# Scores of a two-layer cross-attention block: float32 products replaced by groups of float32r products on high and low parts

## The chip, the cores and the metric

The kernel runs on one core of one Trainium2 chip. The metric is the device time of one execution in microseconds, the median over several executions; lower is better. The core has a matrix engine (TensorE, PE in the profile; its weight loads are PEld), a vector engine (VectorE, DVE), an activation engine (ScalarE, ACT), a general engine (GpSimd, POOL) and SyncE (SP), whose queue issues nearly all of the DMAs here.

## The reference

Two layers, all in float32. Each layer does self attention, cross attention and a gated feed-forward on `x` of 4 x 512 x 320, with 20 heads of 16 dimensions; cross attention reads a context of 4 x 1601 x 192.

```
h1 = _ln(x, n1_g, n1_b)
x = _attn(h1, h1, q1, k1, v1, o1_w, o1_b, heads) + x
h2 = _ln(x, n2_g, n2_b)
x = _attn(h2, context, q2, k2, v2, o2_w, o2_b, heads) + x
h3 = _ln(x, n3_g, n3_b)
a, g = jnp.split(h3 @ ff_w1 + ff_b1, 2, axis=-1)
return a * jax.nn.gelu(g, approximate=False) @ ff_w2 + ff_b2 + x
```

`_attn` is `softmax(q k^T / 4) v` for each head, followed by the output projection.

## The kernel before, in words

**Units.** The work of a layer is cut into units. An attention unit is one batch entry and one group of four heads: 20 units of self attention, then 20 of cross attention, then four feed-forward units (one a batch entry); then the same for the second layer. A self unit has 4 chunks of 128 keys, a cross unit 13 (the last has 65 keys). Units are counted from 0 in order; layer 0 has self units 0 to 19, cross units 20 to 39 and feed-forward units 40 to 43, layer 1 has 44 to 63, 64 to 83 and 84 to 87.

**Rows.** Queries and keys of a unit lie transposed in SBUF, dimensions on partitions. Each head of the four has 32 rows: 16 hold its dimensions, one more holds a constant (keys) or minus the row maximum (queries), so that one product of 32 rows gives `q k - max`. The four heads stand on the four row groups of TensorE, so their products run side by side.

**A chunk** (function `main`). `score` multiplies keys by queries into a PSUM bank (line 1077), ScalarE takes the exponential (line 1083), and one chunk later `values` multiplies by the values (line 1097); ScalarE copies the result out (line 1113) and GpSimd adds it up (line 1114). Between these, the chunk computes part of the row maxima of the unit that follows: `max_pairs` gives products of queries and keys for two heads at a time (line 906, and line 930 for the 65 last keys), and VectorE reduces two banks at once (line 922). One product group for two heads is called here a half round, for all four heads a round. A self unit needs 4 rounds (8 halves), a cross unit 13 (26 halves). When all are there, `max_end` turns the maxima with VectorE (line 970) and eight small DMAs on SP's queue put them in the query rows (line 977).

**Who is served when.** Program order is written by a small planner while the program is built. A clock counts two ticks ("rounds of the clock") a chunk, so unit `u` begins at tick `u.start`, 8 ticks (self) or 26 ticks (cross) after the one before. Side work (projections, normalisation, values, output projection) waits in chains with due times. `steps` runs once at the end of a chunk and takes from the chains what is due and what a credit allows. The chain "slots" holds the transfers that put keys in their rows: `steps` sets `clock["slots"] = 1`, and each entry taken lowers it, so one entry a chunk is taken at most.

**Half rounds of maxima** are handed out by `give`, twice a chunk. It looks at the next two units. If a unit's data has been in place for 3 ticks (`at_hand`), it gives one half round to the chunk. It also counts what is owed: if units would not be done in time, `owed` grows, and each whole unit owed becomes an extra round behind the chunk's own products. Five ticks before a unit begins, what is still left is urgent:

```
if left(v) and (rest == 1 or alone and rest < 1):
    urgent = urgent or v
    owed = max(owed, 1.0 if alone and rest > -4 else (left(v) + 1) // 2)
owed += most * went if total else 0.0
while owed >= 1.0 and any(left(v) for v in ahead) and not (alone and rounds and rest > -4):
```

(`rest` is `v.start - 4 - tick`; `most` is then `(left - 1) / 2`.) Each pass of this loop takes the first unit with something left and calls `at_once(v)`, which projects what is missing and issues the transfers that are still queued.

**Keys of a cross unit** come from `keys_of_context` into a stage, and four queue entries later (lines 773 and 774) by DMA in their rows; queries and the keys of a self unit are put in rows by GpSimd (line 647). Units are projected three ahead (`add_proj`), due at `lead(u) - 6`, where `lead(u)` is the start of the unit before; keys of a cross unit 10 ticks before that. The function `free` keeps a key buffer until its last reader is done.

Of the kernel before, what the change touches and what calls it, by code (L numbers as in the profile page):

```python
# [9 lines left out]
F32 = mybir.dt.float32  # L10
I32 = mybir.dt.int32
# [8 lines left out]
FF = 4 * D  # L20
# [10 lines left out]
HEAD = [0, 2, 1, 3]  # L31
AUG = [DH, DH, 0, 0]
# [34 lines left out]
def kernel(ctx: ExitStack, tc: tile.TileContext, x, context, ws, out):  # L67
# [25 lines left out]
    three = ctx.enter_context(tc.tile_pool(name="three", bufs=3))  # L93
    prs = ctx.enter_context(tc.tile_pool(name="prs", bufs=9))
# [9 lines left out]
    slots = ident.rearrange("p (j s) -> p j s", s=SLOT)  # L104
    keep, ones = [], []
    for b in range(2):
        k, o = (const.tile([P, 1], F32, name=f"{n}{b}") for n in ("keep", "ones"))
        nc.vector.tensor_reduce(k, slots[:, :, b * DH : (b + 1) * DH], AX.XY, ALU.add)
        nc.vector.tensor_reduce(o, slots[:, :, AUG[2 * b]], AX.X, ALU.add)
        keep.append(k)  # L110
        ones.append(o)
# [6 lines left out]
    nmax = []  # L118
    for i in range(2):
        m = const.tile([P, SLOT], F32, name=f"nmax{i}")  # L120
        nc.gpsimd.memset(m, 0.0)
        nmax.append(m)


    kbuf = [const.tile([P, 4 * QT + P], F32, name=f"kT{i}") for i in range(3)]
    qbuf = [const.tile([P, N], F32, name=f"q{i}") for i in range(4)]
    fill = qbuf[3]
    nc.vector.memset(fill, 1.0)

    blank = kbuf[0][:, 4 * QT :]

    def blanks(k):

        n = k.shape[-1] // P
        of = blank.rearrange("p (o w) -> p o w", o=1)
        return [
            lambda a=a, b=min(a + 5, n): dma(
                out=k.rearrange("p (a w) -> p a w", w=P)[:, a:b], in_=of.to_broadcast([P, b - a, P])  # L140
            )
            for a in range(0, n, 5)
        ]


    kept = []
    for b in range(2):
        k = const.tile([P, 1], F32, name=f"kept{b}")
        nc.vector.tensor_scalar(k, keep[b], DH**-0.5, None, ALU.mult)
        kept.append(k)  # L150
    zero = const.tile([P, 1], F32, name="zero")
    nc.vector.memset(zero, 0.0)
    nc.gpsimd.memset(blank, 0.0)
    for b in range(2):
        rows = slice(b * GD, (b + 1) * GD)
        nc.gpsimd.tensor_scalar(blank[rows], blank[rows], zero[rows], ones[b][rows], ALU.mult, ALU.add)
# [16 lines left out]
    wq1, wk1, wv1, wq2 = (wpool.tile([P, 3, D], F32, name=n) for n in ("wq1", "wk1", "wv1", "wq2"))  # L173
# [9 lines left out]
    w1r = wpool.tile([P, FF], F32, name="w1r")  # L183
    w2 = wpool.tile([P, NHC, D], F32, name="w2")
# [57 lines left out]
    def load_ff(l):  # L242
# [5 lines left out]
        def last_rows(half):  # L248
            dma(
                out=w1r[half * REST : (half + 1) * REST, :],  # L250
                in_=ws[l]["ff_w1"][2 * P :, half * FF : (half + 1) * FF],
            )
# [5 lines left out]
            + [lambda c=c: dma(out=w2[:, c], in_=second[:, c]) for c in range(NHC)]  # L258
# [12 lines left out]
    class Unit:  # L271


        def __init__(self, l, kind, b, g):
# [5 lines left out]
            self.cols = [c * P for c in range(self.nch)]  # L280
            if self.cross:
                self.cols = [c % 4 * QT + c // 4 * P for c in range(self.nch - 1)] + [4 * QT]
            self.keyed = False
            self.kslots = deque()
            self.kwhen = None
# [9 lines left out]
            self.pairs = self.hT = self.q = self.kvT = None  # L295
# [15 lines left out]
    for i, u in enumerate(attn):  # L311
# [7 lines left out]
        u.kT = kbuf[(u.m + 1) % 3 if u.cross else 0]  # L319
        u.k0 = 0 if u.cross else u.m % 3 * N  # L320
        u.qbuf = qbuf[3 if u.early else i % 3]
# [327 lines left out]
    def add_proj(u):  # L649
        wq, wk = wq2 if u.cross else wq1, wk1  # L650
# [5 lines left out]
        tiles = [  # L656
            (
                i,
# [796 lines left out]
```

## Time and profile before

| | |
|---|---|
| median of 3 runs | 3196.92 us (3194.64 to 3197.47) |
| span of the profiled execution | 3195.3 us |
| the profiled execution's own time | not given apart from its span; the span lies 1.6 us under the median of the runs |
| busy: PE, PEld, DVE, ACT, POOL | 3163.1, 1466.6, 2069.2, 1972.4, 1204.1 us |
| DMA | 77.84 MB, mean 24 GB/s |

Busy time is the union of an engine's instructions. A float32 matmul stands in the profile as two instructions, each with a weight load of its own, so 2720 scores are 5440 rows. Lines of a view give the source line, the engine, the operation, what it writes and reads, and how often it stands there.

### The profile page before, as it was taken

To read this page: it belongs to the slowest core of one execution; us is meant where nothing else is said; L and a number is where in the kernel's file an instruction comes from. 1 tells how busy PE (TensorE), PEld (TensorE's weight loads), DVE (VectorE), ACT (ScalarE), POOL (GpSimd) and SP (SyncE) were. 2 spreads that over 40 slices of the span, in tenths; PEclk is the share of its full clock that TensorE was granted. 3 is DMA by queue.
4 is the path that set the end of the run, shared out by engine and by line. 5 is a ranking of instruction groups with operands and counts; after the bars stand their busy time and mean duration, and the time that the engine had idled before them with its cause. 6 is when DMAs were issued, how large, how long until landed. Compare 5 with 4: busy or idle time off the path is not lost. (4 is left out here: it accounts for less than half of the span.)

```text
span 3195.3 us, 81370 instructions
## 1 busy us (share of the span) xinstructions
PE 3163.1 (99%) x33970; PEld 1466.6 (46%) x33970; DVE 2069.2 (65%) x2662; ACT 1972.4 (62%) x3951; POOL 1204.1 (38%) x1617
## 2 busy tenths in 40 slices
PE   9999999999999999999999999999999999999999
PEld 4444444444444444355444444444444444443555
DVE  7787777778678677422247777777777777773221
ACT  4666577777777777611147665777778777785110
POOL 5555334443443443301135553344434444432000
PEclk9999999999999999999999999999999999999999
DMA  2220011100100100100012100010010010001000
GB/s 67 56 70 17 14 26 39 33 21 19 33 21 20 33 16 11 39 6 0 1 30 61 34 14 14 22 28 16 16 32 10 16 33 9 16 11 37 9 11 15
DMA packets 104851, 77.84 MB, mean 24 GB/s; under 512 B 42908, under 2 KB 95012, under 8 KB 104484
## 3 DMA queue, kind: packets, MB, share of 16 engines
q1 hardware_dynamic: 104400, 72.63, 9.3%
q8 instruction: 268, 4.39, 0.6%
q14 instruction: 99, 0.81, 0.1%
q0 software_dynamic: 64, 0.00, 0.0%
q10 hardware_dynamic: 20, 0.00, 0.0%
HBM read 33.04 MB, written 7.93 MB: 13 GB/s over the span
## 5 line engine op out<-in xcount | busy, mean ns | idle before, releaser
L1083 ACT ACTIVATE pr<-st 128x512 f32<-128x512 f32 (+1 forms) x2720 | 1408.6, 602 | 420.7 <-PE sps L906 360.4
L1077 PE MATMUL st<-q,kT 32*128 32x512 f32 (+1 forms) x5440 | 1362.6, 614 | 2.6 <-DVE nmax L922 1.7
L922 DVE TENSOR_REDUCE pm<-sps 128x2 f32<-128x1024 f32 (+1 forms) x974 | 1134.4, 1203 | 268.9 <-PE sps L906 262.4
L906 PE MATMUL sps<-kT,q 32*128 32x512 f32 x5120 | 1275.7, 621 | 14.2 <-DVE nmax L922 9.8
L1114 POOL TENSOR_TENSOR o<-o,vo 128x512 f32<-128x512 f32 x576 | 734.5, 1275 | 1375.8 <-ACT vo L1113 1200.7
L1077 PEld LDWEIGHTS st<-q,kT 32*128 32x128 f32 (+1 forms) x5440 | 503.8, 181 | 517.4 <-ACT pr L1083 291.1
L1097 PE MATMUL av<-pr,vals 128*32 128x512 f32 (+1 forms) x5440 | 729.3, 605 | 0.3
L922 DVE TENSOR_REDUCE nmax<-sps 128x2 f32<-128x1024 f32 (+1 forms) x338 | 378.5, 1160 | 151.7 <-PE sps L906 149.1
L906 PEld LDWEIGHTS sps<-kT,q 32*128 32x128 f32 x5120 | 406.1, 183 | 125.8 <-issue 80.6
L1113 ACT COPY vo<-av 128x512 f32<-128x512 f32 x576 | 339.8, 590 | 45.2 <-PE av L1097 41.1
L1097 PEld LDWEIGHTS av<-pr,vals 128*32 128x32 f32 (+1 forms) x5440 | 110.0, 108 | 493.4 <-ACT pr L1083 480.2
L1199 PE MATMUL fps<-hT,w 128*128 128x512 f32 x640 | 286.1, 600 | 1.0 <-DVE kT L1223 0.5
L1222 ACT ACTIVATE gl<-fps,b 128x512 f32<-128x512 f32 x80 | 50.7, 684 | 371.0 <-PE fps L1212 268.0
L647 POOL TENSOR_SCALAR q<-qst,keep,zero 64x128 f32<-64x128 f32 (+1 forms) x476 | 232.3, 488 | 58.9 <-ACT qst L711 25.5
L1199 PEld LDWEIGHTS fps<-hT,w 128*128 128x128 f32 x640 | 119.2, 191 | 152.1 <-issue 146.9
L699 PE MATMUL qps<-hT,wq 112*32 112x128 f32 (+3 forms) x2880 | 126.8, 310 | 0.5 <-DVE pm L922 0.5
L1024 PEld LDWEIGHTS ops<-wo,aT 112*32 112x32 f32 (+1 forms) x3072 | 98.4, 110 | 62.2 <-issue 32.5
L1223 DVE SCALAR_TENSOR_TENSOR hid<-fps,b,gl 128x512 f32<-128x512 f32 x48 | 33.8, 746 | 143.0 <-ACT gl L1222 143.0
L438 POOL TENSOR_SCALAR root<-root 128x4 f32<-128x4 f32 x23 | 5.3, 230 | 315.5 <-DVE root L432 314.8
L1024 PE MATMUL ops<-wo,aT 112*32 112x160 f32 (+1 forms) x3072 | 123.9, 299 | 0.2
L699 PEld LDWEIGHTS qps<-hT,wq 112*32 112x32 f32 (+1 forms) x2880 | 86.7, 110 | 79.3 <-issue 38.8
L1260 DVE TENSOR_TENSOR x<-yps,x 128x320 f32<-128x320 f32 x32 | 15.7, 492 | 148.5 <-PE yps L1253 148.5
(88 smaller groups left out, 2255.7 us busy)
## 6 DMA issues: line engine op xcount, KB each, us to landing
kT<-kst SPq DMA_DIRECT2D x320, 48.0 KB
aT<-o SPq DMA_DIRECT2D x320, 32.0 KB
q<-turned SPq DMA_DIRECT2D x636, 1.0 KB
w<-in_L_xattn_ff_w_dram SPq DMA_DIRECT2D x20, 256.0 KB
ctxT<-ctxT SPq DMA_DIRECT2D x24, 208.0 KB
ctxT<-ctxT SPq DMA_DIRECT2D x12, 416.0 KB
ctxin<-in_ctx_dram SPq DMA_DIRECT2D x24, 192.0 KB
w<-in_L_xattn_ff_w_dram SPq DMA_DIRECT2D x20, 160.0 KB
```

Of the source, the lines that this page charges most:

```text
L647: nc.gpsimd.tensor_scalar(to, stage[rows, :w], keep[b][rows], more[rows], ALU.mult, ALU.add)
L699: nc.tensor.matmul(ps[to, :w], lhsT=wq[:n, k, gs], rhs=first.hT[:n, k, at[i] : at[i] + w], start=(k == 0), stop=(k == 2),)
L906: nc.tensor.matmul(ps, lhsT=u.q[j * SLOT : (j + 1) * SLOT, t * P : (t + 1) * P], rhs=u.kT[j * SLOT : (j + 1) * SLOT, u.k0 + s * 512 : u.k0 ...
L922: nc.vector.tensor_reduce(to[:, j : j + n], part, AX.X, ALU.max, negate=(ns == 1))
L1024: nc.tensor.matmul(ps[f : f + m, : D // 2], lhsT=aT[:n, k, t * P + f : t * P + f + m], rhs=wo[:n, k, cols], start=(k == 0), stop=(k == 2),)
L1077: nc.tensor.matmul(st[:r, :], lhsT=u.kT[rows, u.k0 + u.cols[c] : u.k0 + u.cols[c] + r], rhs=u.q[rows, :], start=True, stop=True)
L1083: nc.scalar.activation(p[:r], st[:r], AF.Exp)
L1097: nc.tensor.matmul(ps[i * SLOT : (i + 1) * SLOT, :], lhsT=columns_of[:r, head : head + SLOT], rhs=pr.pop((c, j))[:r, :], start=True, stop= ...
L1113: nc.scalar.copy(vo, ps)
L1114: nc.gpsimd.tensor_tensor(u.o, u.o, vo, ALU.add)
L1199: nc.tensor.matmul(ps, lhsT=w1[:, k, i * FF + c * P : i * FF + (c + 1) * P], rhs=u.hT[:, k, :], start=ahead and k == 0, stop=not ahead and ...
L1222: nc.scalar.activation(gl, pss[1], AF.Gelu, bias=b1[:, NHC + c : NHC + c + 1])
```

## The change

Queries and keys are cut into two parts each: `high`, rounded to float32r, and `low`, the difference. The 32 rows of a head hold both parts of its 16 dimensions. Keys hold (high, low); queries are held twice, as (high, low) and as (low, high), so that two float32r products give all four part products. Minus the row maximum has moved out of the rows to tiles of its own (`nrows`, two rows a head), which a third float32r product with two rows of ones adds. A score is therefore three products, a product for the maxima two. `round_of` now lays the products of a whole chunk in five steps: heads 0 and 1 have their three scores in steps 0 to 2, heads 2 and 3 in steps 2 to 4, and the products for the maxima fill the other row groups.

The parts reach their rows by way of DRAM: the projection is copied out by ScalarE, GpSimd makes the two parts (`split`), DMAs write them to `q_way` or `k_way`, and DMAs read them back in rows. These are `moves`: five for a self unit (write keys, write queries, read keys, read queries twice), eight for a cross unit. Each move has one entry in the chain "slots". The first two units are moved by hand (`at_once`) before the main loop. Queries and keys of a self unit are projected together (`both`), due at `lead(u) - 9`. A projection waits until earlier moves have left its way buffer (`way_free`). `w1r`, `w2`, the hidden layer and these buffers now share space, and `w2` is loaded later.

```diff
+    def split(low, high):
+        nc.gpsimd.tensor_copy(high.bitcast(F32R), low)
+        nc.gpsimd.tensor_tensor(low, low, high, ALU.subtract)
...
-        due = lead(u) - 6
+        due = lead(u) - 9
         keys_due = due - 10 if u.cross else due
...
+        def move(pairs, then=None, what=None, may=yes):
+            def f():
+                if what:
+                    pending[what] -= 1
+                u.moving = clock["round"]
+                for i, (to, of) in enumerate(pairs):
+                    queue = (nc.sync, nc.scalar, nc.gpsimd)[i % 3] if start["on"] and u.i == 0 else nc.sync
+                    queue.dma_start(out=to, in_=of)
+                if then:
+                    then()
...
+        def way_free(what):
+            return not pending[what] and (len(users[what]) < 2 or not users[what][-2].moves)
...
+        def both(part):
...
+                nc.tensor.matmul(
+                    ps[:, :w],
+                    lhsT=wqk[:n, k, u.g].rearrange("p i d -> p (i d)"),
+                    rhs=first.hT[:n, k, at : at + w],
...
+                nc.scalar.activation(low[:, at : at + w], ps[:, :w], AF.Copy, scale=scales[:, 0:1])
...
+            if u.i:
+                split(low, high)
+            move([(to_k[:, 0], high[GD:]), (to_k[:, 1], low[GD:])], what="q")
+            move([(to_q[:, 0], high[:GD]), (to_q[:, 1], low[:GD]), (to_q[:, 2], high[:GD])], what="q")
+            move([(u.kT[:, u.k0 : u.k0 + N].bitcast(F32), by_rows(to_k))], may=free)
+            read_queries(to_q)
...
+        def add_moves(n, due):
+            for _ in range(n):
+                add(
+                    "slots", 0.0, lambda: u.moves and u.moves.popleft()[0](), due,
+                    lambda: u.moves[0][1]() if u.moves else u.when is not None,
+                    lambda: clock["slots"] > 0 and clock["round"] >= u.moving + 2,
+                )
+        if not u.cross:
+            for part in range(2):
+                add(chain, (0.46,) * 3, lambda part=part: both(part), due - 2 + 2 * part, lambda part=part: part or way_free("q") and way_free("k"))
+            add_moves(5, due)
+        else:
+            add(chain, 2.45, keys_of_context, keys_due, lambda: way_free("k"))
+            add_moves(4, keys_due)
...
+            add(chain, (0.477,) * 3, queries, due - 2, lambda: way_free("q"))
+            add_moves(4, due)
...
+            def product(e):
+                for j, ps in zip(heads, pss):
+                    nc.tensor.matmul(
+                        ps,
+                        lhsT=u.q[j * SLOT : (j + 1) * SLOT, e, t * P : (t + 1) * P],
+                        rhs=u.kT[j * SLOT : (j + 1) * SLOT, u.k0 + s * 512 : u.k0 + (s + 1) * 512],
+                        start=(e == 0),
+                        stop=(e == 1),
+                    )
...
     def max_end(u):
+        nc.vector.tensor_copy(parts[:, :n].bitcast(F32R), u.nm)
+        nc.vector.tensor_tensor(parts[:, n:], u.nm, parts[:, :n], ALU.subtract)
...
-            nc.tensor.matmul(
-                st[:r, :], lhsT=u.kT[rows, u.k0 + u.cols[c] : u.k0 + u.cols[c] + r], rhs=u.q[rows, :], start=True, stop=True
-            )
+            def product(e):
+                nc.tensor.matmul(
+                    st[:r, :],
+                    lhsT=ones[rows.start : rows.start + 2, :r] if e == 2 else u.keys(rows, c),
+                    rhs=u.rows[rows.start : rows.start + 2, :] if e == 2 else u.q[rows, e, :],
+                    start=(e == 0),
+                    stop=(e == 2),
+                )
...
     def at_once(v):
         chain = "early" if v.early else "proj"
-        until(lambda: v.q is not None and v.keyed, chain)
-        while v.kslots:
-            v.kslots.popleft()()
+        while not v.keyed:
+            if not chains[chain][0][2]():
+                for w in attn:
+                    while w.moves and w.moves[0][1]():
+                        w.moves.popleft()[0]()
+            run(chain)
+        while v.moves:
+            f, may = v.moves.popleft()
+            assert may()
+            f()
...
     until(lambda: not chains["proj"], "proj")
+    at_once(units[0])
...
+    at_once(units[1])
+    add_proj(units[2])
```

More of the change, by code (lines that the diff above doesn't have):

```diff
@@ L10 @@
 F32 = mybir.dt.float32
+F32R = mybir.dt.float32r
 I32 = mybir.dt.int32
@@ L28 @@
 GT = GD // SLOT
-HEAD = [0, 2, 1, 3]
-AUG = [DH, DH, 0, 0]
 VW = DH + 1
@@ L146 @@
[L146 to L156, printed above, removed]
+    nmax = [const.tile([P, HG * NQ], F32, name=f"nmax{i}") for i in range(2)]
```

394 lines of the change are left out of this document (195 added, 199 removed).

## The prediction

> **What bounds the kernel now.** I read the page first (engines, slices, chain, groups), the groups with shapes kept apart, then the windows of the self and cross stages, then the timeline of single chunks, last the start of the run, where the planner already does on a small scale what I expect of it here.
>
> ```profile
> span 3195.3 us, 81370 instructions
> PE 3163.1 (99%) x33970; PEld 1466.6 (46%) x33970; DVE 2069.2 (65%) x2662; ACT 1972.4 (62%) x3951; POOL 1204.1 (38%) x1617
> DVE  7787777778678677422247777777777777773221
> ACT  4666577777777777611147665777778777785110
> PEclk9999999999999999999999999999999999999999
> L1077 PE MATMUL st<-q,kT 32*128 32x512 f32 (+1 forms) x5440 | 1362.6, 614 | 2.6 <-DVE nmax L922 1.7
> L906 PE MATMUL sps<-kT,q 32*128 32x512 f32 x5120 | 1275.7, 621 | 14.2 <-DVE nmax L922 9.8
> L922 DVE TENSOR_REDUCE pm<-sps 128x2 f32<-128x1024 f32 x946 | 1117.7, 1219 | 268.9 <-PE sps L906 262.4 <-PE st L1077 0.3
> ```
>
> PE is busy without a break at the full granted clock, and scores and maxima hold most of it. The other engines stand at two thirds overall, but the slices show 70 to 80% in the attention stages. Two windows, between the first and the last turning of maxima in layer 0, with the count of those turnings (one a unit, 16 and 18):
>
> ```profile
> 80.00:380.20 300.20, 295.58 (x3790) 136.23 (x3790) 228.65 (x312) 193.48 (x394) 151.83 (x229) 1.00 0.17 41
> 403.00:1253.80 850.80, 847.21 (x10546) 388.90 (x10542) 633.83 (x736) 643.65 (x1303) 356.49 (x410) 1.00 0.11 25
> 80.00:380.20 300.20, 3.34 (x16) 1.00 0.17 41
> 403.00:1253.80 850.80, 3.81 (x18) 1.00 0.11 25
> ```
>
> After the time come PE, PEld, DVE, ACT, POOL. A self unit takes 300.2/16 = 18.8 us (ACT 12.1, so 3.02 a chunk), a cross unit 850.8/18 = 47.3 us (PE 47.1, DVE 35.2, ACT 35.8, so 2.75 a chunk of 13).
>
> **What a chunk's products cost, before and after.** One chunk of a cross unit:
>
> ```profile
> 900.05 0.19 PEld L1077 LDWEIGHTS st<-q,kT 32*128 32x128 f32 x2 [0.20 <-issue]
> 900.05 0.70 PE L1077 MATMUL st<-q,kT 32*128 32x512 f32 x2
> 900.06 0.19 PEld L906 LDWEIGHTS sps<-kT,q 32*128 32x128 f32 x2
> 900.16 0.19 PEld L1077 LDWEIGHTS st<-q,kT 32*128 32x128 f32 x2
> 900.17 0.19 PEld L906 LDWEIGHTS sps<-kT,q 32*128 32x128 f32 x2
> 900.59 0.59 PE L1077 MATMUL st<-q,kT 32*128 32x512 f32 x2
> 901.03 0.59 PE L1077 MATMUL st<-q,kT 32*128 32x512 f32 x2
> 901.46 0.59 PE L1077 MATMUL st<-q,kT 32*128 32x512 f32 x2
> 901.98 0.16 PEld L1097 LDWEIGHTS av<-pr,vals 128*32 128x32 f32 x8 [0.76 <-ACT pr L1083]
> ```
>
> Four groups of four half products (900.05, 900.59, 901.03, 901.46) start 0.43 us apart once they run, and the values begin 1.93 us after the first. No row shows a float32r product. Its bounds are a quarter of the two halves (0.86/4 = 0.215 us) and a whole half (0.43). I take 0.215: five groups are 1.08 instead of four times 0.43 = 1.72, so 0.65 us less a chunk on PE. The Trainium skill ("FP8 and Floating Point Precision", TensorE Precision Notes) calls true FP32 four passes and a reduced FP32 one that is read whole and truncated; by it a group is a quarter too, and no run here shows it.
>
> The eight loads above begin within 0.12 us and last 0.19 each, so the row groups load side by side, inside the 0.215. The Trainium skill ("TensorE: Matmul & The Clock Gate", LDWEIGHTS) gives columns/1.2 ns for a load whatever its rows; if loads of 128 columns took turns on one path, four would take an estimated 427 ns and a group as long as a half now. The trace does not bear that out.
>
> Where planning stays as it is, a cross unit loses at most 13 x 0.65 = 8.5 us. A chunk without side work gains less:
>
> ```profile
> 57.65 1.68 PE L1077 MATMUL st<-q,kT 32*128 32x512 f32 x8
> 59.46 1.07 PE L1097 MATMUL av<-pr,vals 128*32 128x512 f32 x8
> 60.45 1.16 PE L1077 MATMUL st<-q,kT 32*128 32x512 f32 x5
> 58.81 2.06 ACT L1083 ACTIVATE pr<-st 128x512 f32<-128x512 f32 x4 [0.65 <-PE st L1077]
> 60.73 0.62 ACT L1113 COPY vo<-av 128x512 f32<-128x512 f32 x1
> ```
>
> This chunk of the start has no maxima at all and still lasts 60.45 - 57.65 = 2.80 us, since ACT needs 2.06 + 0.62 for it. A bare chunk with maxima (402.42 to 405.34 below) lasts 2.92, so it gains 0.12, or 1.6 us in a unit of bare chunks. I take the middle of 1.6 and 8.5, 5.1 us, less 0.6 for the maxima's rows: eight issues of 0.50 and 1.9 to land are 5.9 us, and two small operations more on VectorE (0.3, an estimate from the 0.21 us of the turning, 3.81/18), against two chunks of 2.8 before they are read. So -4.5 us a cross unit.
>
> ```profile
> 402.42 0.70 PE L1077 MATMUL st<-q,kT 32*128 32x512 f32 x2
> 405.34 0.70 PE L1077 MATMUL st<-q,kT 32*128 32x512 f32 x2
> L977 SPq DMA_DIRECT2D q<-turned x636: 495/500/701, 29.2 to 2882.8; - x159
> DMA to landing us min/median/max: 1.8/1.9/2.0
> 412.17 2.53 PE L755 MATMUL kps<-ctxT,w 32*64 32x224 f32 x96
> ```
>
> **Small edits at nothing.** The two-part copies on GpSimd replace its copies to rows; ACT makes as many copies out of PSUM as before; VectorE gets two operations of 16 columns a unit. In normal units PE covers all three. Without that cover POOL, at 38%, is the last to matter. The start waits for writes and reads in memory twice: +6 us (bounds 2 and 10, from eight issues and two landings as above). The two units ahead of the feed-forward have no maxima: -3 us.
>
> **The queue of moves is the expensive part.** The chain "slots" gives one entry a chunk. A self unit has 4 chunks and now puts 5 entries in; a cross unit has 13 and puts in 8. An entry whose move was already made by hand stays and uses up a turn. Units 0 and 1 are moved by hand before the loop and leave 10 such entries. So unit 3's entries are the 16th to 20th and come up in chunks 16 to 20, while unit 3 begins at chunk 12. It never recovers: each self unit adds 5 and 4 are taken.
>
> Such a unit has no data `at_hand`, gives no half rounds, and waits for the urgent rule, five ticks before it starts. Then `owed` is (8+1)//2 = 4 plus (8-1)/2 = 3.5: four rounds of the urgent unit and three of the next, which is forced too. So every second self unit carries a flood of 7 rounds in its second chunk, and the other 7 chunks of the pair carry hardly any. For a cross unit it is 13 + 12.5: a flood of 25 rounds in the eleventh chunk of every second unit.
>
> The trace has the same rule at work in its second chunk, with three extra rounds, and what such rounds cost:
>
> ```profile
> 37.83 1.56 PE L1077 MATMUL st<-q,kT 32*128 32x512 f32 x3
> 39.91 7.20 DVE L922 TENSOR_REDUCE nmax<-sps 128x2 f32<-128x1024 f32 x8 [0.68 <-PE sps L906]
> 41.20 1.14 PE L906 MATMUL sps<-kT,q 32*128 32x512 f32 x8 [0.51 <-DVE nmax L922]
> 47.39 0.73 PE L1077 MATMUL st<-q,kT 32*128 32x512 f32 x2
> ```
>
> The chunk lasts 47.39 - 37.83 = 9.6 us. VectorE reduces without a break, and PE waits for it. So a flooded round costs 2 x 1.219 = 2.44 us of VectorE, however fast its products are, and ACT has nothing to do meanwhile.
>
> Where do the floods stop? In layer 0, unit 20+m has its last entry at place 108 + 8m (20 self units of 5, the first cross unit 8, then 8 each) and needs it by about chunk 80 + 13(m-1) - 1.5. That holds from m = 9 on, with m = 7 and 8 partly served. So units 20, 22 and 24 are flooded and 26 by half (14 rounds). In layer 1 the feed-forward stage clears the queue, with 24 calls of `steps` a unit; places are 93 + 8m, in time from m = 6 on, so 64, 66 and 68 are flooded. In the self stages all but the first two units are in floods: 9 pairs a layer.
>
> - A flooded cross pair: 25 x 2.44 = 61.0; the 25 other chunks at 2.80 = 70.0; the wait for the memory path. That is 15 issues of 0.50 and two landings of 1.9 one behind the other, 11.3 us; the projections that the flood forces for the next unit (2.53 for keys) stand ahead of it on PE and cover part, while the transfers, hundreds of KB here, last longer than those of 1 KB. I take 13 (bounds 4 and 20). Sum 144, against 94.6: +49.4, six times: **+296** (bounds 240 and 370). All that is behind the waiting product on PE waits too: values, side work, and so ACT and POOL.
> - Unit 26, half: **+10** (0 to 20).
> - A flooded self pair: 7 x 2.44 = 17.1; 7 chunks at ACT's 3.02 = 21.1; 8 issues and two landings, 7.8. Sum 46.0 against 37.6: +8.4, 18 times: **+151** (55 to 270, path 4 to 12 and chunks 2.8 to 3.4).
> - 25 cross units as planned (12 and 13) at -4.5: **-113** (-200 to -40).
> - Start and last units: **+3**.
>
> 3195.3 + 296 + 10 + 151 - 113 + 3 = 3542. The median of the runs stands 1.6 us over the span: **3544 us**.
>
> On SP's queue, reads stand behind the writes that they wait for, and behind them the rows of maxima and the transfers of outputs; the flood's time holds that, and SP's 15 issues are 7.5 us of a unit's 47.
>
> **Rivals.** (1) The queue keeps pace and no flood comes. Then 38 cross units give -4.5 each, and 38 self units -2.2 (PE loses 4 x 0.65 = 2.6, ACT at 12.1 of 18.8 has room): 3195.3 - 171 - 84 + 3 + 1.6 = 2945 us. For it: PE is the bound in every window. It decides if moves reach rows three ticks before the second half of the unit ahead; the count of 5 entries against 4 chunks speaks against it. (2) Only self units are flooded, and cross units catch up at once: 3195.3 + 151 - 171 + 3 + 1.6 = 3180. Against it is the backlog of 28 and more entries at the first cross unit, which shrinks by 5 a unit. (3) The change does not do what it says: a group takes 0.43 us, by a second pass or loads in turn (the rule above). Flooded stretches are held by DVE and ACT and hardly move; in 25 normal units a chunk costs 5 x 0.43 against 1.72, +5.6 instead of -4.5 us a unit: 3544 + 253 = 3797.
>
> **How the numbers follow.** Forecast 0.78, rival 1 0.13, rival 2 0.03, rival 3 0.06. The ends of all terms together would be 3260 to 3830; they will not fall together, so 3300 to 3790, which leaves out rivals 1 and 2 and most of 3. What can be told from no change is 0.2%, 6.4 us. Faster 0.16 (rivals 1 and 2), same 0.01, slower 0.83.
>
> **What would show it.** Right: DVE and ACT taking turns in the slices of the self stages and the first third of each cross stage; stretches of some 60 us in which VectorE reduces without a break, ACT is idle and PE waits for L922's successor; the maxima's groups with hundreds of us of PE idle before them; cross units of about 43 us late in the stage; score groups 0.215 us apart. Wrong: an even PE at 9 throughout, or cross units alike from first to last (rival 1); groups 0.43 apart (rival 3); a flood's round well under 2.4 us, which would mean that maxima are not held by VectorE.

## The result, and the profile after

The changed kernel takes 4400.9 us (median of 4 runs, 4393.5 to 4412.1) against 3195.9 us for the kernel before on the same chip: a ratio of 1.3775, 95% interval [1.3753, 1.3797]. The forecast was 3544 us, the range 3300 to 3790. The side and the places were right, the size was not: +1205 us instead of +348.

The page of the changed kernel, with the lines that answer to those of before:

```profile
span 4396.0 us, 82324 instructions
PE 3874.0 (88%) x34290; PEld 1896.2 (43%) x34290; DVE 2104.9 (48%) x3113; ACT 1973.4 (45%) x3909; POOL 1124.2 (26%) x1222
DVE  4434452524527776762234344535146376767321
ACT  2334334244255776771123333342443577777411
PEclk7787687557678998999996877775577899999999
L1128 PE MATMUL st<-q,kT 32*128 32x512 f32 (+1 forms) x5440 | 1127.7, 523 | 142.9 <-ACT low L737 63.1
L953 DVE TENSOR_REDUCE pm<-sps 128x2 f32<-128x1024 f32 (+1 forms) x1142 | 1134.5, 1047 | 245.3 <-PE sps L936 211.9
L936 PE MATMUL sps<-kT,q 32*128 32x512 f32 x5120 | 1022.6, 547 | 194.5 <-DMA q<-qway 117.8
```

VectorE and ScalarE work about as long as before, but mostly at 2 to 5 tenths in the self stages and the first third of each cross stage. The maxima's products (L936) now have 194.5 us of idle PE ahead of them, most of it for queries on their way through memory. And the granted clock, 9 in every slice before, falls to 5 to 8 in the same slices. The same in windows: self units 2 to 19, flooded cross units 20 to 25, and cross units 28 to 38 of layer 0 (after the time PE, PEld, DVE, ACT, POOL, the granted clock, DMA share, GB/s):

```profile
102.00:702.70 600.70, 456.79 (x3902) 227.65 (x3902) 265.65 (x456) 220.26 (x443) 128.74 (x151) 0.76 0.20 61
702.70:1271.00 568.30, 502.66 (x3819) 223.10 (x3818) 217.35 (x340) 218.14 (x434) 128.09 (x130) 0.66 0.13 40
1403.40:1929.90 526.50, 500.98 (x6395) 256.72 (x6399) 382.64 (x450) 386.76 (x776) 213.09 (x188) 0.94 0.21 62
```

A flood in a cross unit, the eleventh chunk of unit 20, and the chunk ahead of it, in the timeline (start, duration, engine, operation, idle time before it). A chunk is counted here from its first exponential (L1138) to that of the next:

```profile
749.68 2.06 ACT L1138 ACTIVATE pr<-st 128x512 f32<-128x512 f32 x4 [0.83 <-PE st L1128]
759.02 0.59 ACT L796 COPY stages<-kps 128x224 f32<-128x224 f32 x2 [6.05 <-DMA kway<-stages]
766.64 0.38 ACT L767 ACTIVATE low<-qps 128x256 f32<-128x256 f32 x1 [7.03 <-DMA qway<-low]
767.85 2.65 SPq L690 DMA_DIRECT2D kway<-stages  x4
768.34 2.06 ACT L1138 ACTIVATE pr<-st 128x512 f32<-128x512 f32 x4 [1.32 <-PE st L1128]
772.42 0.80 PE L936 MATMUL sps<-kT,q 32*128 32x512 f32 x4 [3.70 <-DMA q<-qway]
776.07 2.42 DVE L953 TENSOR_REDUCE pm<-sps 128x2 f32<-128x1024 f32 x3 [16.41 <-PE sps L936]
791.43 0.38 ACT L767 ACTIVATE low<-qps 128x256 f32<-128x256 f32 x1 [6.97 <-DMA qway<-low]
791.87 16.17 PE L936 MATMUL sps<-kT,q 32*128 32x512 f32 x62 [4.83 <-ACT low L767]
792.72 18.71 DVE L953 TENSOR_REDUCE pm<-sps 128x2 f32<-128x1024 f32 x24 [3.45 <-PE sps L936]
812.62 28.01 DVE L953 TENSOR_REDUCE pm<-sps 128x2 f32<-128x1024 f32 x36
841.95 2.07 ACT L1138 ACTIVATE pr<-st 128x512 f32<-128x512 f32 x4 [50.13 <-PE st L1128]
```

From 792.72 on it is as forecast: VectorE reduces without a break. The flooded chunk lasts 841.95 - 768.34 = 73.6 us, close to the forecast 61 + 13; those of units 22 and 24 take 60.7 and 71.0. But the chunk ahead of it lasts 768.34 - 749.68 = 18.7 us. The way through memory is made once for each unit of the flood, and the second time waits for the first, part of it in that chunk: the copies out of PSUM (L796, 6.05 us, and L767, 7.03 us) need the staging tiles that the earlier moves still read. The same wait comes once more at 791.43, inside the flood, and PE stands behind it.

### The profile page after: what moved, and what is told of

Read it like the earlier page. It is cut to its first block, busy times and chain, and to the rows that moved or that the text cites. A ratio compares the mean times of both kernels' runs of the same rounds, so it can differ in the third digit from the quotient of the medians.

```text
span 4396.0 us, 82324 instructions
## 1 busy us (share of the span) xinstructions
PE 3874.0 (88%) x34290; PEld 1896.2 (43%) x34290; DVE 2104.9 (48%) x3113; ACT 1973.4 (45%) x3909; POOL 1124.2 (26%) x1222
## 4 chain that ended last, share of the span: by engine, by line
PE 60%; DVE 14%; DMA 11%; ACT 5%; SPq 4%; issue 2%; POOL 2%; POOLq 0%; DVEq 0%; ACTq 0%
PE st L1128 19%; PE av L1152 16%; DVE pm L953 9%; PE fps L1258 6%; ACT pr L1138 4%; DMA qway<-high 4%; PE yps L1312 4%; DVE nmax L953 3%; DMA q<-qway 3%; DMA kway<-stages 3%; PE sps L936 3%; PE ops L1062 2%; PE kps L787 2%; PE vps L878 2%; SPq L690 2%
## 5 line engine op out<-in xcount | busy, mean ns | idle before, releaser
L1138 ACT ACTIVATE pr<-st 128x512 f32<-128x512 f32 (+1 forms) x2720 | 1404.2, 603 | 1098.2 <-PE st L1128 1052.5
L1128 PE MATMUL st<-q,kT 32*128 32x512 f32 (+1 forms) x5440 | 1127.7, 523 | 142.9 <-ACT low L737 63.1
L936 PE MATMUL sps<-kT,q 32*128 32x512 f32 x5120 | 1022.6, 547 | 194.5 <-DMA q<-qway 117.8
L1152 PE MATMUL av<-pr,vals 128*32 128x512 f32 (+1 forms) x5440 | 890.6, 727 | 122.2 <-ACT pr L1138 120.2
L936 PEld LDWEIGHTS sps<-kT,q 32*128 32x128 f32 x5120 | 460.8, 223 | 477.3 <-DVE pm L953 179.3
L953 DVE TENSOR_REDUCE nmax<-sps 128x1 f32<-128x512 f32 (+1 forms) x459 | 381.7, 894 | 565.9 <-PE sps L936 556.6
L1128 PE MATMUL st<-nrows,ones 2*128 2x512 f32 (+1 forms) x2720 | 603.9, 456 | 29.3 <-DMA nrows<-turned 26.6
L1128 PEld LDWEIGHTS st<-nrows,ones 2*128 2x128 f32 (+1 forms) x2720 | 329.5, 215 | 73.7 <-issue 24.0
L1032 DVE STREAM_TRANSPOSE oturn<-o 128x512 f32<-128x512 f32 x80 | 56.3, 704 | 272.2 <-POOL o L1169 272.1
L1312 PE MATMUL yps<-w,hid 128*128 128x320 f32 x640 | 175.3, 434 | 1.3 <-DVE nmax L953 1.3
L1312 PEld LDWEIGHTS yps<-w,hid 128*128 128x128 f32 x640 | 120.7, 190 | 56.9 <-issue 6.1
```

What stands on the lines that cost most here:

```text
L936: nc.tensor.matmul(ps, lhsT=u.q[j * SLOT : (j + 1) * SLOT, e, t * P : (t + 1) * P], rhs=u.kT[j * SLOT : (j + 1) * SLOT, u.k0 + s * 512 : u ...
L953: nc.vector.tensor_reduce(to[:, j : j + n], part, AX.X, ALU.max, negate=(ns == 1))
L1128: nc.tensor.matmul(st[:r, :], lhsT=ones[rows.start : rows.start + 2, :r] if e == 2 else u.keys(rows, c), rhs=u.rows[rows.start : rows.star ...
L1138: nc.scalar.activation(p[:r], st[:r], AF.Exp)
L1152: nc.tensor.matmul(ps[j * SLOT : (j + 1) * SLOT, :], lhsT=columns_of[:r, head : head + SLOT], rhs=pr.pop((c, j))[:r, :], start=True, stop= ...
L1312: nc.tensor.matmul(ps[:, :D], lhsT=hid[c][:, t * P : (t + 1) * P], rhs=w2[:, c, :], start=(c == 0), stop=(c == NHC - 1),)
```

## The experiments

Times by stage, between the first exponentials of units, show where each variant gains or loses (us, layer 0; layer 1 gives the same picture, for the changed kernel 587.1, 559.8 and 517.6 in place of its second, third and fifth row):

| | before | changed | floods alone | products alone | floods and products | mended queue |
|---|---|---|---|---|---|---|
| start to first exponential | 34.2 | 59.1 | 32.4 | 33.0 | 32.3 | 63.2 |
| self units 2 to 19 | 336.1 | 600.7 | 469.0 | 322.5 | 485.8 | 486.2 |
| cross units 20 to 25 | 281.4 | 568.3 | 448.0 | 265.8 | 487.9 | 306.1 |
| cross units 26 and 27 | 94.6 | 132.5 | 91.9 | 90.9 | 86.5 | 103.5 |
| cross units 28 to 38 | 513.4 | 526.4 | 510.5 | 486.0 | 482.4 | 521.0 |
| median of the runs | 3196 | 4400.9 | 3793.5 | 3067.8 | 3829.3 | 3614.2 |

**The queue mended.** The same transfers in 3 and 7 entries a unit, and an entry without a move costs no turn:

```diff
-            move([(to_k[:, 0], high[GD:]), (to_k[:, 1], low[GD:])], what="q")
-            move([(to_q[:, 0], high[:GD]), ...], what="q")
+            move(writes, what="q")
...
-                    "slots", 0.0, lambda: u.moves and u.moves.popleft()[0](), due,
+                    "slots", 0.0, lambda: u.moves.popleft()[0]() if u.moves else clock.update(slots=clock["slots"] + 1), due,
```

> The changed kernel with a queue of moves that keeps pace: a self unit puts in 3 entries instead of 5 and a cross unit 7 instead of 8 (the same transfers, several in one entry), and an entry whose move was already made no longer uses up a turn. Theory A (the floods come from the starved queue and are most of the +1205 us): no stretch of 7 or 25 rounds, even rows of half rounds as before, granted clock above 0.93, cross units 45 to 48 us, time 3080 to 3300 us. Rival B (the way through memory itself is slow: single staging tiles and SP's issues hold ACT and PE in every unit): the floods go, but self units stay above 24 us and the time stays above 3500 us. Rival C (five single-pass groups are slow by themselves): cross units above 50 us, above 3400 us.

3614.2 us, ratio 1.1305 [1.1286, 1.1324]. The cross floods are gone (568.3 to 306.1 us), so the starved queue was their cause. The self floods are gone up to unit 13; units 14, 16 and 18, where the keys of the first cross unit take entries too (by the count alone; no run tests it), still have one (66.2, 51.2 and 42.6 us). But the cross units 28 to 38 are no faster than before (521.0 us for 513.4), and self units 2 to 13 stand at 18 to 30 us, where they took 15 to 22 before. Theory A held for the floods, though not for the time, and B's time held, though not all of its self units stay above 24 us: there is a second cost.

**Floods alone**, on the kernel before:

```diff
     def at_hand(v):
+        if 3 <= v.n % 40 <= 19 or 21 <= v.n % 40 <= 26:
+            return v in forced and clock["round"] >= forced[v] + 3
...
     def at_once(v):
+        forced.setdefault(v, clock["round"])
```

> The kernel before, whose data path and products stay; only the rule for data at hand is withheld for the units that were flooded in the changed kernel (numbers 3 to 19 and 21 to 26 of each layer's 40), until the urgent rule has forced them. This prices the floods without the way through memory and without single-pass products. By the prediction's terms less its memory path: six cross pairs 131 instead of 94.6 us and 18 self pairs 38.2 instead of 37.6, so 3195 + 218 + 11 + 10 = 3435 us. Theory A with the clock as a cost of single-pass products only: 3400 to 3500, granted clock above 0.97. If the clock falls in floods whatever the products are: 3550 to 3800. Rival B (the memory path is most of the cost): below 3350.

3793.5 us, ratio 1.1868 [1.1851, 1.1886]: +597, not +240. The rows of its flood and of the unit behind it:

```profile
575.54 2.07 ACT L1083 ACTIVATE pr<-st 128x512 f32<-128x512 f32 x4 [1.08 <-PE st L1077]
610.13 28.01 DVE L922 TENSOR_REDUCE pm<-sps 128x2 f32<-128x1024 f32 x36
636.43 0.60 ACT L1083 ACTIVATE pr<-st 128x512 f32<-128x512 f32 x1 [38.92 <-PE st L1077]
658.73 2.53 PE L755 MATMUL kps<-ctxT,w 32*64 32x224 f32 x96
661.19 0.86 PE L699 MATMUL qps<-hT,wq 112*32 112x128 f32 x24
540.30:988.30 448.00, 439.08 (x3513) 211.85 (x3514) 220.62 (x333) 214.84 (x434) 120.38 (x149) 0.89 0.08 19
636.40:644.10 7.70, 7.65 (x40) 3.24 (x42) 2.08 (x5) 3.02 (x6) 1.19 (x1) 0.50 0.01 1
648.20:691.90 43.70, 43.26 (x367) 17.28 (x365) 4.49 (x11) 36.73 (x73) 22.49 (x25) 1.00 0.17 42
```

The flooded chunk lasts 636.43 - 575.54 = 60.9 us, against 61.0 forecast (the other two of this layer 58.5 and 62.6). What was left out are the other chunks. A pair is 448.0/3 = 149.3 us instead of 131. Of these 18.3 us, 13.6 stand in the 23 chunks away from the flood, at a granted clock of 1.00: they carry side work (L755, L699 and the like), which stands on PE bare with no product for maxima to hide beside. Another 5.0 stand in the two chunks behind the flood, the first of which takes 7.6 us at a clock of 0.50. So the clock does fall around a flood whatever the products are (0.95 over the run), and the time lies in the range that was given for that, but it is the smaller part.

**Products alone**, on the old data path: three passes a score and two a maximum, each with the same operands (no low parts).

```diff
-                st[:r, :], lhsT=u.kT[rows, ...], rhs=u.q[rows, :], start=True, stop=True
+            def product(e):
+                nc.tensor.matmul(st[:r, :], lhsT=u.kT[rows, ...].bitcast(F32R), rhs=u.q[rows, :].bitcast(F32R), ...)
...
+            return (j,), [lambda e=e: product(e) for e in range(3)], exponential
```

> The kernel before with its own data path (32 rows written by engines, maxima in a row of the queries), but with scores and maxima as float32r products in the order of the changed kernel: three passes a score, two a maximum, each with the same operands (the low parts are left out, so the result is that of truncated operands). This prices the products alone. By the prediction: cross units of about 43 us and self units of 16.6, 2945 to 3000 us. Theory C (single-pass products give nothing, since the clock falls or ACT and the order of a chunk hold): cross units 46 to 48 us and 3100 to 3250 us.

3067.8 us, ratio 0.9596 [0.9581, 0.9610]; clock 0.992. The products do gain, but less than forecast: (513.4 - 486.0)/11 = 2.5 us a cross unit instead of 4.5, and the time lies between the two forecasts. Theory C falls. Chunks with maxima and no side work, which took 2.92 us, now come down to 864.11 - 861.47 = 2.64:

```profile
861.47 2.07 ACT L1107 ACTIVATE pr<-st 128x512 f32<-128x512 f32 x4 [0.92 <-PE st L1097]
864.11 2.06 ACT L1107 ACTIVATE pr<-st 128x512 f32<-128x512 f32 x4
```

ScalarE, which also copies a result out in each, has no gap there: it holds such a chunk now, not PE.

**The order of a bare chunk.** In the changed kernel a chunk without maxima has all four heads in lockstep. Its rows, first at full, then at half clock:

```profile
1070.93 1.45 PE L1128 MATMUL st<-q,kT 32*128 32x512 f32 x7
1074.30 1.68 PE L1128 MATMUL st<-q,kT 32*128 32x512 f32 x8
1076.03 2.06 ACT L1138 ACTIVATE pr<-st 128x512 f32<-128x512 f32 x4 [0.82 <-PE st L1128]
874.67 2.06 ACT L1138 ACTIVATE pr<-st 128x512 f32<-128x512 f32 x4 [1.31 <-PE st L1128]
879.28 1.08 ACT L1138 ACTIVATE pr<-st 128x512 f32<-128x512 f32 x2 [1.31 <-PE st L1128]
851.60:911.50 59.90, 55.73 (x261) 16.89 (x260) 2.77 (x8) 34.42 (x65) 15.25 (x13) 0.50 0.10 26
```

3.37 us (1070.93 to 1074.30) at full clock, 4.61 (874.67 to 879.28) in unit 21, which runs at half clock from end to end; 2.80 was forecast. The edit:

```diff
         free = [0] * HG
+        if len(made) == HG and all(len(rows) == 1 for rows, _, _ in made):
+            free[2:] = [3, 3]
```

> The changed kernel in which, in a chunk without maxima, heads 2 and 3 start their scores after the three passes of heads 0 and 1, as they do when maxima go along. Theory: all four heads in lockstep keep the exponentials from starting until the fourth bank is free, which makes a bare chunk 3.37 us at full clock; with the change it falls to 2.8 to 2.95 at full clock. About 280 bare chunks lie in flooded stretches: 60 to 170 us less, 4230 to 4340 us. Rival (a bare chunk is held by PE at half clock, whatever the order): less than 20 us, time above 4380.

4296.6 us, ratio 1.3441 [1.3421, 1.3461]: 104 us less, as the theory had it. A bare chunk falls to 2.65 us at full clock and, in unit 21, to 4.27 at half clock.

**Rows of maxima on GpSimd's queue** (on the mended queue): `queue = ... if start["on"] else nc.gpsimd`. What it goes against, a first chunk of a cross unit with the mended queue:

```profile
850.71 8.44 SPq L1015 DMA_DIRECT2D nrows<-turned  x8
860.35 0.80 PE L1128 MATMUL st<-nrows,ones 2*128 2x512 f32 x2 [5.19 <-DMA nrows<-turned]
856.00:860.00 4.00, 0.00 (x0) 0.00 (x0) 0.44 (x1) 0.00 (x0) 0.56 (x1) 0.77 0.12 39
860.00:868.00 8.00, 7.65 (x84) 5.15 (x88) 2.01 (x3) 3.08 (x7) 1.26 (x1) 0.50 0.40 107
```

> The kernel with the mended queue (3614 us), and the eight transfers of a unit's rows of maxima issued on GpSimd's queue instead of SyncE's, where they stand among the moves. Theory: a unit's first products of rows wait for transfers that come late because SP is issuing moves (one measured: eight issues in 8.44 us, PE idle 5.2 us, then some 8 us at half clock); on another queue cross units fall from 48.1 to about 45 us and self units by 1 to 2: 3420 to 3520 us. Rival (the staging tiles and the way through memory hold the units, not the queue): 3580 to 3630.

3759.0 us, ratio 1.1761 [1.1744, 1.1779]: 145 us worse, a miss for the theory and the rival alike:

```profile
861.80 4.51 POOL L1015 DMA_DIRECT2D nrows<-turned  x8
871.41 0.79 PE L1128 MATMUL st<-nrows,ones 2*128 2x512 f32 x2 [5.56 <-DMA nrows<-turned]
L1128 PE MATMUL st<-nrows,ones 2*128 2x512 f32 (+1 forms) x2720 | 649.1, 435 | 183.2 <-DMA nrows<-turned 177.5 <-issue 5.6
```

The wait for rows became 177.5 us; with SP it was 44.9. The issue itself is not slower (4.51 us for eight, where SP took 8.44 above), and it begins 0.7 us after the rows are turned (median; 0.1 with SP), behind GpSimd's other work. Most of the loss comes after it: the waiting product begins 871.41 - 866.31 = 5.1 us after the last issue, on SP's queue 860.35 - 859.15 = 1.2 us. Over all waits it is 1.3 to 7.2 us against 1.1 to 2.1. Why transfers from GpSimd's queue land later here is not shown.

**A second pair of staging tiles** for odd self units (on the mended queue):

```diff
         def staged():
+            if not u.cross and u.n % 2 and u.m > 3:
+                return (room[n][:, :N] for n in ("low", "high"))
```

> The kernel with the mended queue (3614 us), and a second pair of staging tiles for odd self units from the fifth on (room that is used by keys of the cross stage). Theory: a projection's copy out of PSUM waits on ScalarE for the move that still reads the single staging tile (102 us, and 66 us of PE behind it), and exponentials wait behind it; with two pairs self units fall from 22 to 23 us to about 20: 3500 to 3560 us. Rival (they wait for the rows of maxima and for the latency of the way, not for staging): 3600 to 3620.

3583.5 us, ratio 1.1211 [1.1194, 1.1227]: 31 us less, between the two. All of these together, with the order:

> Mended queue, rows of maxima on GpSimd's queue, second staging pair for odd self units, and heads 2 and 3 after heads 0 and 1 in chunks without maxima. If the parts add up: 3280 to 3430 us, granted clock above 0.95. If what is left is the latency of the way itself (write, read, rows at hand three ticks later): above 3450.

3724.1 us, ratio 1.1653 [1.1631, 1.1675]: 3614 + 145 - 31 = 3728, so the measured parts add up without a gain from the order, and the queue of GpSimd spoils it. Both ranges had counted on a gain from that queue.

**Holding the clock** (on the changed kernel): each first pass made three times where PE has little to do.

```diff
-            return heads, [lambda e=e: product(e) for e in range(2)], reduce
+            return heads, [lambda e=e: product(e) for e in ((-1, -1, 0, 1) if start["both"] else (0, 1))], reduce
...
-            return (j,), [lambda e=e: product(e) for e in range(3)], exponential
+            return (j,), [lambda e=e: product(e) for e in range(-2, 3)], exponential
```

(a pass below 0 is the first one, started and stopped by itself; chunks with maxima drop theirs)

> The changed kernel as it was, floods included, with products that change nothing: in a flooded round and in a chunk without maxima each head's first pass is made three times, each time from the start. At full clock this adds 0.43 us a bare chunk where it is not hidden, and nothing to a flooded round, which VectorE holds. Theory (half clock in and after floods is a cost of its own, because PE's single-pass products leave it too little to do): granted clock rises from 0.82 to above 0.93, bare chunks go from 4.6 to about 3.4 us, time 4100 to 4300 us. Rival (the clock follows the waits and costs little): clock stays below 0.87 and the time is 4400 to 4600 us.

4454.3 us, ratio 1.3950 [1.3926, 1.3974]. Unit 21 does return to full clock and its chunks to 3.8 us:

```profile
880.00:920.00 40.00, 35.19 (x291) 13.97 (x291) 0.00 (x0) 26.97 (x54) 12.84 (x10) 1.00 0.05 14
```

and the unit is 7.1 us shorter (52.8 for 59.9), but the same passes make a bare chunk that had the full clock 0.47 us longer (3.84 for 3.37), and flooded chunks stay as they were (74.7 us for 73.6 in unit 20). The mean clock rose to 0.887, between the two expectations, and the time is in the rival's range. So raising the clock in this way won nothing; what the half clock costs by itself this run does not tell, since its passes have a price of their own. More work for PE restored the clock in unit 21. The Trainium skill ("TensorE: Matmul & The Clock Gate", Part 1: The HAM clock gate) says that a monitor of how busy PE has been lets 4 or 8 of 8 pulses through. The trace agrees with 0.50 and 1.00 here, and with 0.50 for the 8 us behind the idle gap above; but the busy share of the profile does not tell which it will be, since unit 21 of the changed kernel stayed at 0.50 with PE busy for 55.73 of 59.90 us.

**Moves made earlier** (on the changed kernel): for both units of a flood, three ticks ahead.

```diff
+            if not alone and ahead and left(ahead[0]) and ahead[0].start - 4 - clock["round"] == 4:
+                for v in ahead:
+                    if not v.early:
+                        at_once(v)
```

> The changed kernel, floods as they are, but the moves that a flood would force are made three ticks earlier, by hand, for both units that the flood serves (in the first chunk of a self unit, in the tenth of a cross unit). Theory (inside a flood the products wait one behind the other for projection, write, read and landing): flooded self chunks fall from 28 to about 20 us and flooded cross chunks from 73 and 61 to about 62, 150 to 220 us in all: 4180 to 4260 us. Rival (the same waits only move into the chunk before, since ScalarE and PE are in order and the staging tiles are single): less than 60 us, above 4340.

4652.5 us, ratio 1.4571 [1.4546, 1.4595]: 252 us worse. The theory fails; the rival named the waits that only move, but no loss. The flooded chunk of unit 20 became longer, 91.0 us for 73.6, and the wait ahead of it only moved forward by a chunk (23.9 us in place of 18.7). The run shows the price of the way in a cross unit where nothing hides it:

```profile
1097.91 5.36 SPq L690 DMA_DIRECT2D kway<-stages  x4
1120.20 1.21 SPq L690 DMA_DIRECT2D q<-qway  x2
1126.78 0.42 PE L964 MATMUL sps<-kT,q 32*128 32x66 f32 x2 [24.42 <-DMA q<-qway]
```

From the first write to the first product are 1126.78 - 1097.91 = 28.9 us, and PE is idle for 24.4 of them.

**The second staging pair under floods**:

> The changed kernel, floods as they are, with a second pair of staging tiles for odd self units from the fifth on. Theory: in a self flood the second unit's projection waits on ScalarE until the first one's moves have read the single pair (133 us in all), and PE and the exponentials behind it: 80 to 140 us less, 4260 to 4320 us. Rival (these waits overlap with others): less than 30 us, above 4370.

4439.3 us, but with this edit the kernel computes other values, so nothing is read from its time.

**Rows a chunk earlier** in cross units (mended queue and second staging pair): `c == u.nch - (4 if u.cross else 3)`, with the planner's 4 ticks made 6.

> The kernel with the mended queue and the second staging pair (3584 us); in cross units the last maxima of the next unit are due one chunk earlier, and its rows are turned and sent a chunk earlier. Theory (the 3 us a cross unit by which this lies above the same products on the old data path, 47.9 against 44.2, are the wait for rows that stand behind moves on SP, and the half clock after it): 34 cross units at -2.5 to -3.5: 3465 to 3500 us. Rival (they are the moves' traffic and the order of work, not this wait): above 3560.

3549.1 us, ratio 1.1106 [1.1084, 1.1127]: 34 us less, where 85 to 120 were expected. It gained (507.7 - 491.8)/11 = 1.4 us a cross unit in layer 1 and 1.0 in layer 0. PE's wait for the rows of maxima is gone, so that wait was not the whole of the 3 us.

**One pass instead of five groups** on the old path:

> The kernel before with its own data path, and scores and maxima as one float32r pass each instead of three and two (the low parts are left out: operands are truncated). It shows what is left when products cost a quarter: three groups of 0.215 us less a chunk than with five. If PE stays the bound: 13 x 0.65 = 8.4 us a cross unit and 2.6 a self unit less than the 3068 us of the five-group variant, 2650 us. If ScalarE and VectorE (35.8 and 35.2 of 47.3 us) come next: about 40 us a cross unit, 2850 to 2950 us. If PE then has too little to do and its clock falls to half: 3000 us and more.

2950.2 us, ratio 0.9229 [0.9207, 0.9250]: the fastest of all, at the price of operands without their low parts. A normal cross unit is 41.9 us; VectorE at 386 and ScalarE at 380 of 461 us come near PE, whose granted clock is 0.93:

```profile
486.00:947.00 461.00, 430.38 (x4976) 196.16 (x4968) 386.40 (x471) 380.14 (x790) 220.61 (x266) 0.93 0.11 27
```

**Floods and products together, without the way**, and the same with the order mended:

> The kernel before with both: data at hand withheld for the same units as in the run with floods (3793 us), and scores and maxima as float32r products in the changed kernel's order as in the run with products alone (3068 us; the low parts are left out). All that is missing to the changed kernel (4401 us) is the way through memory. If floods and products add up: 3793 - 129 = 3665 us, and the way is worth 735. Theory (single-pass products make flooded stretches worse, by lockstep in bare chunks, 104 us by the order run, and by half clock): 3750 to 3850 us, granted clock below 0.90, and the way is worth 550 to 650. Rival (the clock is the larger part): above 3950 us, the way below 450.

> The same, with heads 2 and 3 after heads 0 and 1 in chunks without maxima. Theory: lockstep costs the same 80 to 110 us here as in the changed kernel. Rival (it cost there only because chunks ran at half clock behind the waits of the way): below 40 us.

3829.3 us, ratio 1.1980 [1.1960, 1.2000], and 3677.5 us, ratio 1.1509 [1.1492, 1.1526]. The first is in the range of its theory (the clock, at 0.904, just above). Lockstep costs 152 us here, more than the 80 to 110 expected. With it mended ScalarE goes on without a gap, 788.39 to 791.03 = 2.64 us a chunk:

```profile
788.39 2.06 ACT L1109 ACTIVATE pr<-st 128x512 f32<-128x512 f32 x4 [0.64 <-PE st L1099]
791.03 2.06 ACT L1109 ACTIVATE pr<-st 128x512 f32<-128x512 f32 x4
```

**Loads and outputs on GpSimd's queue** (on the 3549 us variant), so that SP keeps moves and rows:

> The kernel with mended queue, second staging pair and earlier rows (3549 us); weight and context loads, and the transfers of divided outputs, are issued on GpSimd's queue instead of SyncE's, so that SP keeps the moves and the rows of maxima. Theory (without floods, what the way costs is mostly the queue of SP, which issues some 17 us of transfers in a self unit of 19 to 25, each in order behind the waits of the others): self units fall by 2 to 4 us, cross units by 1: 3400 to 3470 us. Rival (it is the latency of write, read and staging inside a self unit's 8 ticks, whatever the queue): above 3530.

3548.3 us, ratio 1.1098 [1.1080, 1.1117]: no change. Loads and outputs on SP's queue are not what holds the units there; whether the moves and rows that stay on it hold each other is not shown.

## Why the prediction was right in direction and wrong in size

**The account.** From 3196 us: floods alone +597 (3793.5); single-pass products inside them +36 (3829.3), which is -116 by the products and +152 by lockstep; the way through memory, +572 (4400.9), with which come the low parts, the earlier due times and the later loads of `w2`. Without most floods the way costs nearly the same: 3614.2 - 3067.8 = 546.

**Right.** The places of the floods (units 2, 4, ... 18, then 20, 22, 24 and 26 by half; in layer 1 units 64, 66, 68), their 7 and 25 rounds, VectorE as their bound, with 58.5 to 62.6 us a cross flood (floods alone) for 61.0; a group in one pass: with the mended queue, at full clock, one begins 0.23 us after the other where it does not wait (forecast 0.215), and two more passes a head, two groups, make a bare chunk 0.47 us longer, so rival 3 (0.43 a group) is out. Rival 1 needed a queue that keeps pace, and rival 2 cross units that catch up at once; neither came.

```profile
849.27 0.39 PE L1128 MATMUL st<-q,kT 32*128 32x512 f32 x2
849.50 0.40 PE L1128 MATMUL st<-q,kT 32*128 32x512 f32 x1
```

**Wrong, the price of other chunks in a flooded pair** ("the 25 other chunks at 2.80 = 70.0", "7 chunks at ACT's 3.02"). The first is a chunk without side work, the second ScalarE's busy time alone; the side work of PE is in neither. The prediction's own rows had it: a normal cross unit is 47.3 us, its 13 chunks at 2.92 only 38.0, so 9.3 us of a unit are side work, and 18.8 - 12.1 = 6.7 in a self unit. Twice these, 18.6 and 13.4 a pair, is near what the floods alone lie above the sum: 149.3 - 131 = 18.3, and 469.0/9 - 38.2 = 13.9. That 18.6 comes so near is partly chance, since only 13.6 of the 18.3 are side work and 5.0 are the chunks behind the flood, with their lower clock. Over 6 and 18 pairs that is 360 us, the largest error.

**Wrong, the order inside a bare chunk.** 2.80 us was read from a chunk in which heads 0 and 1 went ahead; the new `round_of` puts four heads in step. With the half clock that follows, and less what the products gain there, cross pairs are (487.9 - 448.0)/3 = 13.3 us longer than with floods alone, self pairs 1.9: 114 us.

**Wrong, the way through memory.** 13 us a cross pair and 7.8 a self pair were its price. Measured are (568.3 - 487.9)/3 = 26.8 and (600.7 - 485.8)/9 = 12.8 in layer 0, 23.7 and 12.0 in layer 1, some 157 us over the price in all. The price was for a wait inside the flooded chunk, and there it was enough in cross units: of the 26.8 us only 4.9 are in that chunk, 8.8 are in the chunk ahead of it and 13.1 in the other chunks of the pair. A flood goes the way twice, and the second time waits for the staging tile of the first. In a self flood (unit 4), whose first two chunks take 11.8 and 29.2 us where they take 3.4 and 21.6 without the way:

```profile
176.22 0.84 ACT L737 ACTIVATE low<-qkps,scales 128x256 f32<-128x256 f32 x2 [7.05 <-DMA qway<-low]
181.88 0.80 PE L936 MATMUL sps<-kT,q 32*128 32x512 f32 x4 [3.12 <-DMA q<-qway]
185.50 2.42 DVE L953 TENSOR_REDUCE nmax<-sps 128x2 f32<-128x1024 f32 x3 [24.98 <-PE sps L936]
192.25 14.05 DVE L953 TENSOR_REDUCE nmax<-sps 128x2 f32<-128x1024 f32 x18 [3.42 <-PE sps L936]
```

The prediction counted issues and landings once and let the projection of the next unit cover them; that projection is itself what waits.

**Wrong, normal units** at -4.5 us. That was the middle between a gain held by ScalarE (1.6) and one held by PE (8.5). Products gave -2.5, near ScalarE's bound, and the way, which the sum had at 0.6 for its rows and at nothing for its moves, took back (526.4 - 486.0)/11 = 3.7: 25 units at +1.2 instead of -4.5, some 140 us. The same window with products alone, to set beside that of units 28 to 38 above:

```profile
750.10:1236.20 486.10, 473.42 (x6726) 256.95 (x6726) 374.82 (x430) 389.57 (x792) 214.41 (x234) 0.99 0.10 24
```

PE is idle 25.5 us instead of 12.7 there, 7.8 of it for rows of maxima, and busy 27.6 us longer, at a mean clock of 0.94 instead of 0.99. What brings the clock down in these units was not tested. The start took 24.9 us instead of 6, units 26 and 27 37.9 instead of some 6. These terms together are 824 of the 857 us.

**What stays open.** The mended variants still lie some 480 us over the products on the old path (3549 against 3068). Three floods a layer, the start and rows are part of it; a second staging pair gave 31 us, earlier rows 34, a freer SP nothing. That the rest is the latency of write, read and staging within the 8 ticks of a self unit is argued, not shown. Open too are why transfers from GpSimd's queue land later, why earlier moves made floods longer, what the moves' traffic does (51 GB/s over the run for 24 before), and what the half clock costs by itself: all runs that changed it changed the work as well.

## What to carry to other kernels

A path that a planner hides is priced twice: with its cover, and at its own length when the cover starves; count the entries per unit against the turns per unit before looking at durations. When a chunk loses the work that ran beside it, price it as the whole unit less that work, side work included, not as the shortest chunk of the trace. Where the next engine is close behind, take its bound and not the middle. An edit that speeds up the bounding engine is worth measuring on the old data path first: here that alone was 4% faster and the path to feed it 18% slower.

## What the runs showed of the hardware that was not expected

In the changed kernel the granted clock stayed at 0.50 for a whole unit (21) of 59.9 us in which the profile has PE busy for 55.7. With three times the first passes it came back to 1.00 in the third chunk of that unit; with the same floods and float32 products it was 1.00 from the unit's first chunk. Eight transfers of 2 KB took 8.44 us to issue on SP, right behind moves, where others took 4.54. Transfers of the same size issued on GpSimd's queue kept PE waiting 1.3 to 7.2 us after their last issue, on SP's 1.1 to 2.1. From the first write to DRAM to the first product on the data read back, a cross unit took 28.9 us, though two landings of small transfers are 1.9 us each.
